# Row 1's front issued beside row 0's products, two rows' gating on GpSimd, and row steps placed at other times, in a kernel of time mixing and routed experts on one core

## The chip, the cores and the metric

The kernel runs on one core of one Trainium2 chip. The metric is the time of one execution on the device in microseconds; the median of three runs stands for a kernel. The engines are TensorE (PE; its weight loads are PEld), VectorE (DVE), ScalarE (ACT), GpSimd (POOL) and SyncE (SP, which issues most of the transfers).

## What is computed

The input x is 16 rows of 512 tokens with 256 channels, in float32. Two layers follow each other, both of the form x + layernorm(layer(layernorm(x))):

```python
x = x + layernorm(attn(layernorm(x)))
x = x + layernorm(ffn(layernorm(x)))
```

The first layer (attn) shifts a quarter of the channels by one token forward and a quarter backward, mixes this with the unshifted tokens in three ways, projects to k, v and r, and runs a recurrence over the tokens:

```python
eku = exp(u + kt); out = (a + eku * vt) / (b + eku)
ek = exp(kt);      a, b = a * ew + ek * vt, b * ew + ek
...
return (sigmoid(r) * out) @ Wo.T
```

The second layer (ffn) routes each token to the best two of eight experts (gate by softmax, 256 channels to 256 hidden, silu(x w1 + b1) * (x w3 + b3), then w2), and adds a shared expert with 512 hidden channels that every token goes through.

## The kernel before, in words

A row (b = 0 to 15, 512 tokens, 256 channels) is the unit of the first layer. The tokens lie in four tiles of 128, the channels in two halves of 128. The work of a row has a front and a back, each a list of named steps; a third kind of work fills in between.

**The front** (`front`, L289): `sum` and `sq` (L293 to L316) find mean and variance of the tokens: for row 0 on DVE, for the others on ACT with accumulated sums, with small operations on POOL (`scales`, L263). `xn` normalises on ACT (L278, called from L318). `pt` transposes on PE (L284) and ACT copies to `xx` (shifted) and `x1` (L329 to L332). `mix` makes `d`, `mk`, `mv`, `mr` on DVE (L334 to L341). `k0` and `k1` (`kv`, L356) each project k and v for one half of the channels (PE L346, two matmuls of 512 columns each), take exp of k on ACT (`ek`, L364), multiply by v on DVE (`ekv`, L366) and run two scans on DVE (`sb`, `sa`, L371), whose first columns POOL sets to zero. `r` projects r and takes exp on ACT (`er`, L352). `d0` and `d1` (`divide`, L374) are two DVE operations and a reciprocal (L379) for one half; `f0` and `f1` (`finish`, L381) are one DVE operation and the product `g` (L384).

**The back** (`back`, L395): `po0` and `po1` multiply g by Wo, 8 matmuls each (L406), with the statistics on DVE (`st_b`, L253). `x2` normalises on ACT and POOL adds x (L421). `stc` takes the statistics of the sum (`st_c`) and POOL makes the scales. `xr` normalises on ACT into a tile that also holds gate weight and destination of each token; `pu` transposes that tile (PE) and ACT copies it to `xT`; `pl` and `pg` (L461, L473) make the gate's logits and turn them; the top two and the counts follow on DVE (L479 to L494); `pc` (L499) ranks the tokens on PE, DVE makes their places in a buffer in HBM (L502 to L515), and POOL scatters the rows there with 8 indirect transfers (L520). `sel` chooses the blocks of 256 tokens of one expert that are full by then.

**What fills in between.** `shared` (L722) is the shared expert of one row in six steps: four of two times four matmuls of 512 columns (`hs_pa`, `hs_pb`, L734) and two of `pz` (L749). An expert block is pushed through a pipeline (`push`, L704): the block is loaded, turned (`px`, L648), multiplied by w1 and w3 (`pa`, `pb`, L662), gated on ACT (`sil`, L665) and DVE (`he`, L667), multiplied by w2 (`pq`, L678), biased on DVE (`ye`, L682), weighted on ACT and scattered by POOL (L691). A push of one block does px of that block, pq of another and pa, pb of the first. BESIDE says how many shared steps go beside each of the first rows.

**What sets the order.** PE, DVE, ACT and SP execute their instructions in the order in which the program writes them (`manual_schedule`, L106); POOL's are chained to the same order by `pool()` (L143). The program collects every step with a time and calls the steps sorted by that time (`at`, `in_order`, L889 to L895). Row b begins at START[b] or PERIOD behind the one before; `ROW` gives the offset of each step of any row, `ROWS` what is other for single rows (L32, L33). `CONST_AT` places a step that makes small constants (`the_constants`, L206: iota on POOL, casts and memsets on DVE), `WHOLE_AT` one that scales three weights (`whole_weights`, L237). The times are no microseconds: only the order that they give matters. Behind the last row's front comes the tail: remaining blocks, shared steps at the times in FILL, and the end of each half row (`fetch`, `gather`, `conclude`, `put`; K_FIRST and K_LAST place them), which reads the experts' results, adds, normalises and writes out.

**Tiles.** The pool `wk` has one buffer for each tag (`d`, `mk`, `mv`, `mr`, `xx`, `xn`, `g`, `ek0`, `sb0` and so on; `hs0` and `hs1` belong to the shared expert), so that a row's tile must be read to its end before the next row's is written. Three x tiles are in turn. PSUM is a pool of eight banks that all products share.

Of the kernel before, what the change touches and what calls it, by code (L numbers as in the profile page):

```python
# [8 lines left out]
F32 = mybir.dt.float32  # L9
# [19 lines left out]

PERIOD = 10.0  # L30
START = [0.0, 10.0, 20.0, 30.0, 40.0]
ROW = {'x': -7.6, 'sum': -5.31, 'sq': -4.3, 'xn': -1.7, 'pt': -0.59, 'mix': 0.8, 'r': 3.2, 'k0': 2.61, 'k1': 2.82, 'd0': 3.51, 'f0': 7.4, 'd1': 7.41, 'f1': 7.42, 'po0': 9.6, 'po1': 12.6, 'x2': 12.91, 'stc': 12.92, 'xr': 17.9, 'pu': 19.21, 'pg': 19.52, 'pc': 20.43, 'sel': 21.5, 'pl': 19.22}  # L32
ROWS = {1: {'x': -8.3, 'sum': -5.6, 'sq': -4.51, 'xn': -2.5, 'pt': -1.99, 'mix': 0.0, 'r': 6.0, 'd0': 6.01, 'f1': 9.8, 'po0': 11.4, 'po1': 12.4, 'x2': 14.11, 'stc': 14.21, 'xr': 18.1, 'pu': 19.91, 'pg': 20.33, 'pc': 20.84, 'sel': 20.85, 'pl': 20.22}, 3: {'xn': -0.1, 'pt': 0.01, 'mix': 1.3, 'f0': 7.0, 'd1': 7.01, 'f1': 8.3, 'po0': 11.39, 'po1': 11.4, 'x2': 11.41, 'stc': 11.42, 'xr': 16.0, 'pu': 17.61, 'sel': 21.2, 'pl': 17.92}, 0: {'x': -7.1, 'sum': -5.11, 'sq': -1.1, 'xn': -1.09, 'pt': -1.08, 'mix': -1.07, 'r': 6.6, 'k0': -0.29, 'k1': 0.12, 'd0': 6.61, 'f0': 6.62, 'd1': 6.63, 'f1': 7.6, 'po0': 12.59, 'x2': 12.71, 'stc': 12.72, 'xr': 17.6, 'pu': 19.31, 'pg': 20.32, 'pc': 21.83, 'sel': 21.84, 'pl': 19.32}, 2: {'sq': -3.51, 'xn': -3.5, 'd0': 3.71, 'f0': 5.9, 'd1': 5.91, 'f1': 7.2, 'po0': 10.6, 'po1': 11.6, 'x2': 11.91, 'stc': 12.52, 'xr': 16.6, 'pu': 16.91, 'pc': 20.23, 'sel': 21.2, 'pl': 16.92}}  # L33
CONST_AT = 8
WHOLE_AT = -3.8
X_PARTS = 2
VSTATS = 1
LEAD = 1
TURN_FIRST = True
PHASE = 0.2  # L40
BESIDE = [9, 6, 5, 2]
EARLY = 7
LAST_BESIDE = 6
XR_COPY = "pool"
HALVES_AT = 2.5
FILL = [-0.7, 0.7, 1.2, 13.5, 14.0, 15.5]
Z_AFTER = [2, 3]
K_FIRST = 1.0
K_LAST = 32.4
FINE = 2  # L50
FETCH = 4.8
# [13 lines left out]
def kernel(  # L65
# [30 lines left out]


    full = [max(0, -((E * (BS - 1) - 2 * T * (b + 1)) // BS)) for b in range(B)]
    LEFT = (2 * N - E) // P + E - 2 * full[B - 2]
    SINGLE = E - 1  # L100
    PAIRS = -((SINGLE - LEFT) // 2)
# [187 lines left out]
    def front(b):  # L289
# [32 lines left out]
        def turn():  # L322
            xn = it.pop("xn")
            p0 = it["p0"] = transposed(xn, 0, f"pt0_{b}")
            p1 = transposed(xn, 1, f"pt1_{b}")
            xx = it["xx"] = wk.tile([P, T], F32, tag="xx", name=f"xx{b}")
            pool(nc.gpsimd.memset(xx[:H, 0:1], 0.0))
            pool(nc.gpsimd.memset(xx[H:P, T - 1 : T], 0.0))
            nc.scalar.copy(xx[:H, 1:T], p0[:H, 0 : T - 1])  # L329
            nc.scalar.copy(xx[H:P, 0 : T - 1], p0[H:P, 1:T])  # L330
            x1 = it["x1"] = wk.tile([P, T], F32, tag="x1", name=f"x1_{b}")
            nc.scalar.copy(x1, p1)  # L332

        def mix():  # L334
            d = wk.tile([P, T], F32, tag="d", name=f"d{b}")
            nc.vector.tensor_tensor(d, it["p0"], it["xx"], ALU.subtract)
            it["m"] = {}
            for n, c in (("k", C_MK), ("v", C_MV), ("r", C_MR)):
                m = wk.tile([P, T], F32, tag=f"m{n}", name=f"m{n}{b}")
                nc.vector.scalar_tensor_tensor(m, d, colt[:, c : c + 1], it["xx"], ALU.mult, ALU.add)  # L340
                it["m"][n] = m  # L341

# [38 lines left out]
        def finish(o):  # L381
            ek, ekv, sa, sb = w[o]
            nc.vector.scalar_tensor_tensor(sa, ekv, eu[:, o : o + 1], sa, ALU.mult, ALU.add)
            nc.vector.tensor_mul(gs[b][:, o, :], sa, sb)  # L384

        return dict(
            sum=sums, sq=squares, xn=norm, pt=turn, mix=mix, r=receptance, k0=lambda: kv(0), k1=lambda: kv(1),
# [710 lines left out]
```

## Time and profile before

| what | value |
|---|---|
| median of 3 runs | 1077.15 us (1076.97 to 1079.2) |
| the profiled execution's own time | 1082.54 us |
| its span | 1080.8 us |
| PE busy | 1012.6 us (94%), 4202 matmuls |
| PEld busy | 701.4 us (65%) |
| DVE busy | 769.2 us (71%) |
| ACT busy | 541.5 us (50%) |
| POOL busy | 569.2 us (53%) |
| mean granted clock of PE | 0.979 |

A span is the time from the first to the last instruction; the execution's own time lies 1.7 us around it. Starts in the timeline are microseconds from the span's start. A row of the timeline is start, duration of the group, engine, line, operation, output and inputs, shape, the count of instructions in the group (xN), and in brackets the idle time before it with what released the engine. The granted clock is the share of the full TensorE clock, 1.00 or 0.50 at any moment, as a mean over the stretch asked for.

### The profile page before, as it was taken

The page shows a single profiled execution, that of the slowest core. Times are in us where ns is not written, and L with a number is a line of the kernel's source. Part 1 is how long each engine was busy: PE and PEld are TensorE (multiplying, and loading weights), DVE is VectorE, ACT ScalarE, POOL GpSimd, SP SyncE. Part 2 cuts the span into 40 slices and gives each one's busy share as a digit, 9 for nine tenths or more (in the row PEclk, how much of TensorE's full clock was granted, in tenths as well). Part 3 has the DMA queues.
Part 4 walks back from the last instruction along what each step waited for, and adds up shares of the span by engine and source line. Part 5 has one row for each costly group of instructions (what it writes and reads, how often), then busy time and mean ns, then how long its engine had stood idle before and what let it go on. Part 6 is the DMA issues. An engine that isn't in the chain of part 4 may idle for free.

```text
span 1080.8 us, 15095 instructions
## 1 busy us (share of the span) xinstructions
PE 1012.6 (94%) x4202; PEld 701.4 (65%) x4202; DVE 769.2 (71%) x1905; ACT 541.5 (50%) x1150; POOL 569.2 (53%) x858
## 2 busy tenths in 40 slices
PE   5769898999999999999999999989999999999996
PEld 2335454767777677866768676667667878556554
DVE  4897696887797888878888887866353222478864
ACT  3355463657557484755757566543423333333341
POOL 2336435174656547465654646554442222369885
PEclk9789999999999999999999999989999999999998
DMA  4011313436465554645556464543556766879943
GB/s 161 6 39 38 112 71 126 151 120 192 146 200 159 175 186 154 215 153 169 154 184 189 163 192 156 171 162 119 164 196 217 246 217 207 282 246 314 314 143 114
DMA packets 80900, 181.68 MB, mean 168 GB/s; under 512 B 9597, under 2 KB 45583, under 8 KB 80816
## 3 DMA queue, kind: packets, MB, share of 16 engines
q1 hardware_dynamic: 67360, 144.89, 42.0%
q0 software_dynamic: 12736, 34.77, 8.7%
q10 hardware_dynamic: 720, 1.06, 0.3%
q8 instruction: 33, 0.54, 0.2%
q14 instruction: 51, 0.42, 0.1%
HBM read 123.12 MB, written 58.47 MB: 168 GB/s over the span
## 4 chain that ended last, share of the span: by engine, by line
PE 67%; issue 5%; ACT 4%; DVE 3%; POOL 3%; DMA 2%; SPq 0%; DVEq 0%; POOLq 0%; ACTq 0%
PE pq L678 10%; PE pa L662 9%; PE pz L749 8%; PE hs_pa L734 8%; PE pb L662 8%; PE hs_pb L734 7%; PE po L406 4%; PE pv L346 3%; PE pk L346 3%; PE pr L346 3%; PE px L648 2%; POOL xbuf L520 1%; DVE he L667 1%; PE pt L284 1%; ACT xr L278 1%
## 5 line engine op out<-in xcount | busy, mean ns | idle before, releaser
L691 POOL DMA_INDIRECT ybuf<-ye,xg x135 | 137.5, 1019 | 235.2 <-ACT ye L689 176.1
L520 POOL DMA_INDIRECT xbuf<-xr,place x128 | 134.7, 1052 | 94.3 <-DVE rest L515 46.7
L678 PE MATMUL pq<-we,he 128*128 128x256 f32 x540 | 134.2, 391 | 12.6 <-DVE he L667 11.8
L662 PE MATMUL pa<-xgT,we 128*128 128x256 f32 (+1 forms) x568 | 130.0, 372 | 0.0
L667 DVE SCALAR_TENSOR_TENSOR he<-pb,we,sil 128x256 f32<-128x256 f32 (+1 forms) x142 | 60.0, 463 | 96.7 <-PE pb L662 59.6
L662 PE MATMUL pb<-xgT,we 128*128 128x256 f32 (+1 forms) x568 | 128.3, 369 | 0.0
L734 PE MATMUL hs_pa<-xT,ws1t 128*128 128x512 f32 x256 | 120.6, 593 | 0.0
L734 PE MATMUL hs_pb<-xT,ws3t 128*128 128x512 f32 x256 | 120.3, 592 | 0.0
L678 PEld LDWEIGHTS pq<-we,he 128*128 128x128 f32 x540 | 97.6, 193 | 31.2 <-DVE he L667 17.4
L665 ACT ACTIVATE sil<-pa,we 128x256 f32<-128x256 f32 (+1 forms) x142 | 58.0, 460 | 117.7 <-PE pa L662 77.9
L749 PE MATMUL pz<-ws2t,hs 128*128 128x256 f32 x512 | 115.8, 380 | 0.2 <-DVE hs L740 0.2
L662 PEld LDWEIGHTS pa<-xgT,we 128*128 128x128 f32 x568 | 106.1, 193 | 14.2
L662 PEld LDWEIGHTS pb<-xgT,we 128*128 128x128 f32 x568 | 104.1, 190 | 13.2
L749 PEld LDWEIGHTS pz<-ws2t,hs 128*128 128x128 f32 x512 | 96.7, 190 | 19.8 <-issue 5.7
L379 DVE RECIPROCAL sb<-sb 128x512 f32<-128x512 f32 x32 | 107.3, 3353 | 1.1
L734 PEld LDWEIGHTS hs_pb<-xT,ws3t 128*128 128x128 f32 x256 | 48.6, 190 | 61.2 <-issue 56.7
L740 DVE SCALAR_TENSOR_TENSOR hs<-hs_pb,colt,hs_s 128x512 f32<-128x512 f32 x64 | 46.5, 733 | 51.9 <-PE hs_pb L734 21.7
L734 PEld LDWEIGHTS hs_pa<-xT,ws1t 128*128 128x128 f32 x256 | 48.3, 190 | 43.7 <-issue 40.1
L278 ACT ACTIVATE acc<-acc,nb_d,rs_d 128x256 f32<-128x256 f32 x64 | 34.9, 593 | 81.1 <-POOL nb_d L273 80.9
L682 DVE TENSOR_TENSOR ye<-pq,we 128x512 f32<-128x512 f32 (+1 forms) x71 | 46.7, 658 | 36.1 <-PE pq L678 31.8
L364 ACT ACTIVATE ek<-pk 128x512 f32<-128x512 f32 x32 | 18.9, 597 | 102.3 <-PE pk L346 53.7
L406 PE MATMUL po<-wa,g 128*128 128x256 f32 x256 | 63.1, 391 | 5.0 <-DVE g L384 4.9
(187 smaller groups left out, 1868.7 us busy)
## 6 DMA issues: line engine op xcount, KB each, us to landing
we<-in_we SPq DMA_DIRECT2D x71, 898.0 KB
xg<-xbuf SPq DMA_DIRECT2D x64, 258.0 KB
in<-ybuf SPq DMA_DIRECT2D x32, 512.0 KB
x<-in_x SPq DMA_DIRECT2D x15, 512.0 KB
out<-acc SPq DMA_DIRECT2D x30, 256.0 KB
x2s<-x SPq DMA_DIRECT2D x14, 512.0 KB
inx<-x2s SPq DMA_DIRECT2D x19, 256.0 KB
zs<-z SPq DMA_DIRECT2D x9, 512.0 KB
```

The source lines that it names most:

```text
L346: nc.tensor.matmul(p, w[:, c, o * P : (o + 1) * P], r, start=(c == 0), stop=(c == NC - 1))
L379: nc.vector.reciprocal(sb, sb)
L406: nc.tensor.matmul(p[:, i, :], g[:, c, t * P : (t + 1) * P], woT[:, c, :], start=(c == 0), stop=(c == NC - 1))
L520: i = nc.gpsimd.indirect_dma_start(out=xbuf[:, :], out_offset=bass.IndirectOffsetOnAxis(ap=place[:, t, k : k + 1], axis=0), in_=xr[k][:, t ...
L662: nc.tensor.matmul(p[:, f, :], w[:, k : k + P], xgT[:, c, :], start=(c == 0), stop=(c == NC - 1))
L665: nc.scalar.activation(s[:, f, :], pp[0][:, f, :], AF.Silu, bias=w[:, O_B1 + f : O_B1 + f + 1])
L667: nc.vector.scalar_tensor_tensor(h[:, f, :], pp[1][:, f, :], w[:, O_B3 + f : O_B3 + f + 1], s[:, f, :], ALU.add, ALU.mult)
L678: nc.tensor.matmul(p[:, t, :], h[:, f, t * P : (t + 1) * P], w[:, k : k + C], start=(f == 0), stop=(f == NF - 1))
L682: nc.vector.tensor_tensor(y, p, w[:, None, O_B2 : O_B2 + C].to_broadcast([P, n, C]), ALU.add)
L691: j = nc.gpsimd.indirect_dma_start(out=ybuf[:, :], out_offset=bass.IndirectOffsetOnAxis(ap=xg[:, t, R_TO : R_TO + 1].bitcast(U32), axis=0) ...
L734: nc.tensor.matmul(p, w[:, c, f * P : (f + 1) * P], xT[:, c, :], start=(c == 0), stop=(c == NC - 1))
L749: nc.tensor.matmul(p[:, i, :], h[f][:, t * P : (t + 1) * P], ws2t[:, f, :], start=(f == 0), stop=(f == NS - 1))
```

## The change

Row 1's `sum`, `sq`, `xn`, `pt` and `mix` are issued before row 0's `r` and `d0`, where only its `sum` and `sq` were before; its `k0` and `k1` go ahead of row 0's `po0` and `po1`, behind which they were. Since row 0's `mk`, `mv`, `mr`, `xx` are still being read then, row 1 has tiles of its own for them, with the tags `hs0` and `hs1`, which the shared expert does not use yet. For rows 0 and 1 the product `g` (four instructions) is issued on POOL instead of DVE (`G_POOL`). The constants are made before the weights are scaled, at the start, not behind row 0's products.

The other numbers place steps anew. Each x is loaded one place earlier. In row 1's back, shared steps stand between `pg` and `pc`, and `pl`, `pg` follow `pu` without row 3's `pt` between; in row 2's, `pg` and `pc` stand directly behind each other and ahead of a shared step that was between them before. In rows 4 to 14 `x2` and `stc` of the row before go ahead of `k1`, and `f0` goes ahead of an expert block; the order on PE is the same there. Row 15's `r` and `d0` come two time units later, so that on DVE two blocks' `ye` and `he` stand ahead of its division, and on ACT two loads of a function table are added. In the tail one shared step comes one push earlier, `pc` of row 15 stands behind both `pz` of one row instead of between them, and a few of the first gathers are 0.2 earlier. `FIRST_CHOICE` is 0 and changes nothing.

```diff
@@ -29,23 +29,25 @@
 
 PERIOD = 10.0
 START = [0.0, 10.0, 20.0, 30.0, 40.0]
-ROW = {'x': -7.6, 'sum': -5.31, 'sq': -4.3, 'xn': -1.7, 'pt': -0.59, 'mix': 0.8, 'r': 3.2, 'k0': 2.61, 'k1': 2.82, 'd0': 3.51, 'f0': 7.4, 'd1': 7.41, 'f1': 7.42, 'po0': 9.6, 'po1': 12.6, 'x2': 12.91, 'stc': 12.92, 'xr': 17.9, 'pu': 19.21, 'pg': 19.52, 'pc': 20.43, 'sel': 21.5, 'pl': 19.22}
-ROWS = {1: {'x': -8.3, 'sum': -5.6, 'sq': -4.51, 'xn': -2.5, 'pt': -1.99, 'mix': 0.0, 'r': 6.0, 'd0': 6.01, 'f1': 9.8, 'po0': 11.4, 'po1': 12.4, 'x2': 14.11, 'stc': 14.21, 'xr': 18.1, 'pu': 19.91, 'pg': 20.33, 'pc': 20.84, 'sel': 20.85, 'pl': 20.22}, 3: {'xn': -0.1, 'pt': 0.01, 'mix': 1.3, 'f0': 7.0, 'd1': 7.01, 'f1': 8.3, 'po0': 11.39, 'po1': 11.4, 'x2': 11.41, 'stc': 11.42, 'xr': 16.0, 'pu': 17.61, 'sel': 21.2, 'pl': 17.92}, 0: {'x': -7.1, 'sum': -5.11, 'sq': -1.1, 'xn': -1.09, 'pt': -1.08, 'mix': -1.07, 'r': 6.6, 'k0': -0.29, 'k1': 0.12, 'd0': 6.61, 'f0': 6.62, 'd1': 6.63, 'f1': 7.6, 'po0': 12.59, 'x2': 12.71, 'stc': 12.72, 'xr': 17.6, 'pu': 19.31, 'pg': 20.32, 'pc': 21.83, 'sel': 21.84, 'pl': 19.32}, 2: {'sq': -3.51, 'xn': -3.5, 'd0': 3.71, 'f0': 5.9, 'd1': 5.91, 'f1': 7.2, 'po0': 10.6, 'po1': 11.6, 'x2': 11.91, 'stc': 12.52, 'xr': 16.6, 'pu': 16.91, 'pc': 20.23, 'sel': 21.2, 'pl': 16.92}}
-CONST_AT = 8
-WHOLE_AT = -3.8
+ROW = {'x': -9.6, 'sum': -5.31, 'sq': -4.3, 'xn': -2.2, 'pt': -0.59, 'mix': 0.9, 'r': 3.2, 'k0': 2.61, 'k1': 2.82, 'd0': 3.51, 'f0': 6.4, 'd1': 7.41, 'f1': 7.42, 'po0': 9.6, 'po1': 12.6, 'x2': 12.81, 'stc': 12.82, 'xr': 17.8, 'pu': 19.11, 'pg': 19.42, 'pc': 20.43, 'sel': 21.4, 'pl': 19.12}
+ROWS = {1: {'x': -11.09, 'sum': -11.08, 'sq': -11.07, 'xn': -10.56, 'pt': -9.61, 'mix': -9.6, 'r': 5.0, 'k0': 1.71, 'k1': 1.82, 'd0': 5.11, 'f0': 7.0, 'd1': 7.01, 'f1': 9.5, 'po0': 11.1, 'po1': 12.4, 'x2': 14.11, 'stc': 14.21, 'xr': 17.8, 'pu': 19.61, 'pg': 19.73, 'pc': 20.24, 'sel': 20.25, 'pl': 19.72}, 3: {'xn': -0.4, 'pt': 0.01, 'mix': 1.3, 'f0': 7.0, 'd1': 7.01, 'f1': 8.3, 'po0': 11.39, 'po1': 11.4, 'x2': 11.41, 'stc': 11.42, 'xr': 16.0, 'pu': 17.61, 'sel': 21.2, 'pl': 17.92}, 0: {'x': -7.1, 'sum': -5.61, 'sq': -1.6, 'xn': -1.59, 'pt': -1.58, 'mix': -1.07, 'r': 3.6, 'k0': -0.29, 'k1': 0.12, 'd0': 3.61, 'f0': 3.62, 'd1': 3.63, 'f1': 7.6, 'po0': 12.59, 'x2': 12.71, 'stc': 12.72, 'xr': 17.6, 'pu': 19.31, 'pg': 20.32, 'pc': 21.83, 'sel': 21.84, 'pl': 19.32}, 2: {'x': -7.3, 'sum': -5.01, 'sq': -3.21, 'xn': -3.2, 'd0': 3.41, 'f0': 5.6, 'd1': 5.61, 'f1': 6.9, 'po0': 10.8, 'po1': 11.7, 'x2': 12.01, 'stc': 12.42, 'xr': 16.5, 'pu': 17.31, 'pg': 19.92, 'pc': 20.03, 'sel': 21.0, 'pl': 17.32}, 15: {'r': 5.2, 'd0': 5.51}}
+CONST_AT = -4
+WHOLE_AT = -1.8
 X_PARTS = 2
 VSTATS = 1
 LEAD = 1
 TURN_FIRST = True
 PHASE = 0.2
 BESIDE = [9, 6, 5, 2]
+G_POOL = 2
+FIRST_CHOICE = 0
 EARLY = 7
 LAST_BESIDE = 6
-XR_COPY = "pool"
+XR_COPY = 'pool'
 HALVES_AT = 2.5
-FILL = [-0.7, 0.7, 1.2, 13.5, 14.0, 15.5]
+FILL = [-0.7, 0.7, 1.2, 12.5, 14.0, 15.5]
 Z_AFTER = [2, 3]
-K_FIRST = 1.0
+K_FIRST = 0.8
 K_LAST = 32.4
 FINE = 2
 FETCH = 4.8
@@ -96,6 +98,9 @@
 
 
     full = [max(0, -((E * (BS - 1) - 2 * T * (b + 1)) // BS)) for b in range(B)]
+    for b in range(B - 1):
+        if b < FIRST_CHOICE:
+            full[b] = 0
     LEFT = (2 * N - E) // P + E - 2 * full[B - 2]
     SINGLE = E - 1
     PAIRS = -((SINGLE - LEFT) // 2)
@@ -323,7 +328,11 @@
             xn = it.pop("xn")
             p0 = it["p0"] = transposed(xn, 0, f"pt0_{b}")
             p1 = transposed(xn, 1, f"pt1_{b}")
-            xx = it["xx"] = wk.tile([P, T], F32, tag="xx", name=f"xx{b}")
+            if b == 1:
+
+                two = [wk.tile([P, 2, T], F32, tag=f"hs{i}", name=f"row1_{i}") for i in range(2)]
+                it["own"] = [two[i // 2][:, i % 2, :] for i in range(4)]
+            xx = it["xx"] = it["own"][3] if b == 1 else wk.tile([P, T], F32, tag="xx", name=f"xx{b}")
             pool(nc.gpsimd.memset(xx[:H, 0:1], 0.0))
             pool(nc.gpsimd.memset(xx[H:P, T - 1 : T], 0.0))
             nc.scalar.copy(xx[:H, 1:T], p0[:H, 0 : T - 1])
@@ -335,8 +344,8 @@
             d = wk.tile([P, T], F32, tag="d", name=f"d{b}")
             nc.vector.tensor_tensor(d, it["p0"], it["xx"], ALU.subtract)
             it["m"] = {}
-            for n, c in (("k", C_MK), ("v", C_MV), ("r", C_MR)):
-                m = wk.tile([P, T], F32, tag=f"m{n}", name=f"m{n}{b}")
+            for i, (n, c) in enumerate((("k", C_MK), ("v", C_MV), ("r", C_MR))):
+                m = it["own"][i] if b == 1 else wk.tile([P, T], F32, tag=f"m{n}", name=f"m{n}{b}")
                 nc.vector.scalar_tensor_tensor(m, d, colt[:, c : c + 1], it["xx"], ALU.mult, ALU.add)
                 it["m"][n] = m
 
@@ -381,7 +390,10 @@
         def finish(o):
             ek, ekv, sa, sb = w[o]
             nc.vector.scalar_tensor_tensor(sa, ekv, eu[:, o : o + 1], sa, ALU.mult, ALU.add)
-            nc.vector.tensor_mul(gs[b][:, o, :], sa, sb)
+            if b < G_POOL:
+                pool(nc.gpsimd.tensor_tensor(gs[b][:, o, :], sa, sb, ALU.mult))
+            else:
+                nc.vector.tensor_mul(gs[b][:, o, :], sa, sb)
 
         return dict(
             sum=sums, sq=squares, xn=norm, pt=turn, mix=mix, r=receptance, k0=lambda: kv(0), k1=lambda: kv(1),
```

## The prediction

> **What bounds the kernel now.** I read the page's slices first, then the table by stretches, the waits of PE, and the timeline where a wait is long.
>
> ```profile
> PE   5769898999999999999999999989999999999996
> PEclk9789999999999999999999999989999999999998
> ```
>
> A digit is a fortieth of the span, 27 us. PE is full in nearly every slice; the thin ones are the first three or four, one after 700 us, and the last. Stretches (start:end, length, PE, PEld, DVE, ACT, POOL busy, then the granted clock):
>
> ```profile
> 0.00:27.00 27.00, 15.42 (x32) 6.88 (x32) 12.96 (x31) 10.54 (x29) 6.01 (x25) 1.00 0.49 161
> 27.00:54.00 27.00, 19.04 (x48) 10.45 (x48) 23.55 (x42) 9.92 (x24) 8.66 (x15) 0.75 0.01 5
> 54.00:81.00 27.00, 16.37 (x69) 9.89 (x68) 24.41 (x58) 13.68 (x28) 8.49 (x19) 0.81 0.12 38
> ...
> 300.00:400.00 100.00, 98.70 (x465) 71.85 (x464) 83.36 (x206) 62.53 (x138) 58.76 (x87) 1.00 0.57 177
> ...
> 712.00:716.00 4.00, 0.00 (x0) 0.00 (x0) 4.00 (x3) 0.15 (x1) 2.99 (x5) 0.92 0.09 33
> 716.00:720.00 4.00, 3.74 (x9) 3.02 (x10) 0.60 (x2) 1.23 (x3) 2.21 (x3) 0.50 0.41 120
> ```
>
> In 27 to 81 DVE is busy (24 of 27 us), not PE: row 0's chain runs alone. From the first shared product (73.53) PE is the bound (98.7 of 100), and whatever DVE, ACT or POOL save there buys nothing unless PE waits for it. PE executes the same matmuls after the change, and the same set stands ahead of the first shared product. So the time moves by three things only: when the first shared product starts, how long PE waits after it, and how long its clock is halved (0.50 above, behind a wait). PE's waits after 80 us (total, times, longest):
>
> ```profile
> PE pq L678 <- DVE he L667: 11.8, 24, 4.3
> PE pr L346 <- ACT x L278: 4.4, 1, 4.4
> PE pl L461 <- ACT xT L446: 3.9, 14, 0.8
> PE pg L473 <- ACT lg L469: 2.2, 3, 1.4
> PE pc L499 <- DVE sc L494: 1.1, 1, 1.1
> ```
>
> The two waits of 4.3 and 4.4 us, and the row-1 waits of pg and pc, are all that steps of named rows can win.
>
> **1. The front, up to 73.53.** The path, start and duration:
>
> ```profile
> 26.75 0.72 DVE L377 SCALAR_TENSOR_TENSOR sb<-ek,eu,sb 128x512 f32<-128x512 f32 x1
> 28.31 3.35 DVE L379 RECIPROCAL sb<-sb 128x512 f32<-128x512 f32 x1
> ...
> 38.41 0.69 DVE L384 TENSOR_TENSOR g<-sa,sb 128x512 f32<-128x512 f32 x1
> ...
> 39.16 5.14 PE L406 MATMUL po<-wa,g 128*128 128x256 f32 x14 [4.92 <-DVE g L384]
> ...
> 48.51 4.35 POOL L421 TENSOR_TENSOR x<-x,x 128x512 f32<-128x512 f32 x2 [1.06 <-ACT x L278]
> ```
>
> - *ACT.* Row 1's sums (1.7 from 22.60), squares (2.1), normalising (2.1) and POOL's scales between them now precede row 0's exp ek: 20.8 instead of 18.14. Its product ekv waited for pv until 20.35 anyway, so DVE's scans of row 0 end 27.25 instead of 26.83: +0.4.
> - *Row 1's mix* (0.69+0.75+0.75+0.74, 2.8 with overlap) now precedes row 0's division: its first stt starts at about 30.05, +3.3. The constants' casts and memsets (39.02 to 40.17, 1.1) go to the start, beside DVE's wait for weights; without that cover they cost 1.1.
> - *g on POOL.* Division and finishing took 26.75 to 39.10. Without two multiplies of 0.65 they take 11.05, to 41.1. A POOL multiply of this size is not in the trace; nearest is POOL's add (L421, same shape): median 1.27, 2.17 each in the row above, where DVE's scan of two SBUF inputs runs beside (2.22 against 1.20 alone). DVE runs row 1's scans here now. Bounds 1.27 to 2.2: g at 42.5 to 43.3.
> - The Trainium skill, "SBUF — State Buffer", section "Who interferes with whom", speaks against this edit: a DVE instruction with two SBUF inputs and a GpSimd instruction reading SBUF exclude each other. By it part 1 ends at its upper end, which is rival A below; the slowed pair agrees.
> - *po, statistics.* Row 1's ekv and scans (2×2.87) go ahead of the statistics, to 46.9, beside POOL's g and po (5.8 us at half clock). po ends at 48.3, the statistics at 49.3 to 50 (45.5 before).
> - *Given back.* Those scans no longer run beside the two adds of x2: 1.27 each instead of 2.17. Row 0's second statistics end at 56.0 to 56.7, not 54.06.
> - From there the chain (scales, row 2's squares and normalising, xr, pu, pl, pg, top-2, pc) took 19.47; 18.4 to 19.5 now, row 1's g being out of it. First shared product 74.4 to 76.2. **Taken: +1.8**; bounds −2 (DVE's 2.8 us of multiplies all come back) to +4.5 (upper POOL price, po wholly at half clock).
>
> **2. Row 1's pl, pg, pc (108 to 123).** The waits for pg (1.42) and pc (1.07) get shared products or transposes in front of them. pl now waits for xT behind row 3's normalising on ACT (1.7), pg 0.5. Counting from pu to the third shared step: 122.79 becomes 121.45. **−1.3** (0 to −2.5). The windows there show clock 1.00, so no clock comes back.
>
> **3. Row 3's r (182 to 187).** pr waits 4.42 for ACT's normalising of x2, which frees PSUM banks, which waits for POOL's nb_b, behind eight scatters (168.63 to 178.96). What counts is when row 2's places are ready. Row 2's pg and pc move ahead of a shared step, so DVE makes the places earlier; a new wait of some 2.7 us appears between pg and pc, the top-2 (112.64 to 115.40 for row 1) being uncovered, but POOL's chain ends 1.8 to 2 us sooner against PE's work. The 4.42 shrinks accordingly, and the half-clock stretch behind it (0.66 in 182:187, worth 1.7) goes or moves. px, 187.20 before, comes 3.55 sooner, of which part 2 is 1.3. **−2.25** (−4 to +0.8, where both waits stay).
>
> **4. Rows 4 to 14.** PE's order is the same. On DVE and ACT x2's statistics go ahead of the second scan pair, f0 goes ahead of an expert block's he, and each x load (512 KB) goes ahead of the block loads' SP instructions of a place or two; PE waits for a load once only in the whole run (px for xg, 1.0 us), so this costs nothing, or up to 1 us where it pushes such a load. f0 (0.65+0.69) goes into time in which DVE waited for pb (59.6 us, 26 times). PE's bank releases move: pk's and pv's banks 4 to 6 us later. **0**; bounds −2 to +7.
>
> **5. Row 15's division (711 to 730).**
>
> ```profile
> 711.92 3.35 DVE L379 RECIPROCAL sb<-sb 128x512 f32<-128x512 f32 x1
> ...
> 715.74 0.86 DVE L667 SCALAR_TENSOR_TENSOR he<-pb,we,sil 128x256 f32<-128x256 f32 x2
> 716.26 3.78 PE L678 MATMUL pq<-we,he 128*128 128x256 f32 x8 [4.34 <-DVE he L667]
> 719.83 3.06 PE L662 MATMUL pa<-xgT,we 128*128 128x256 f32 x8
> ```
>
> The division (0.72+0.69+3.35) stands ahead of he. Afterwards he is ahead of it, but behind row 14's statistics (2.75) and the scans moved behind them; he at about 714.3, pq at 714.85, gap 2.6. Before, the clock was halved 715.6 to 722.5, which costs 3.4 of PE work; behind the shorter gap 0 to 1.7. The next pq waits 0.65 more. pu comes at 726.35, not 730.54. ACT reloads a table twice more (1.28), off the path. **−4.2** (−1 to −6).
>
> The Trainium skill, "TensorE: Matmul & The Clock Gate", section "What's actually happening", lets the clock fall after an idle window of about 3.4 us: by it 2.6 us would leave the clock whole, which is rival E below. The trace does not bear it out: a wait of 2.19 us ending at 806.88 was followed by a clock of 0.63 (808:812), so I go by that row.
>
> **6. Tail.** One shared step moves by a push, pc.15 behind a pz, some gathers by 0.2: **0** (±1). The 10 us behind the last matmul stay.
>
> **Sum:** 1.8−1.3−2.25+0−4.2+0 = −5.95. The profiled execution took 1082.54 (span 1080.8), so 1076.6. The unprofiled median, 1077.15, is 5.4 lower; PE's order is the same in both, so I take the difference over: **1071.2**.
>
> **Rivals.**
> - *A: the front costs more* (POOL's g at 2.2, po at half clock): +4.5 instead of +1.8: 1073.9. For: scans run beside g. Against: adds are shortened by the same edit. 0.12.
> - *B: row 15's wait is only shortened* and the clock stays halved as long: −1.4 instead of −4.2: 1074.0. For: the row at 806.88. 0.14. A and B together 1076.7: 0.08.
> - *C: the front gains* (DVE, busy 24 of 27 us, loses 2.8 us of multiplies): −2: 1067.4. Against: row 0's division waits for row 1's mix. 0.10.
> - *D, slower:* in rows 4 to 14 f0's 1.34 us on DVE delays he, and PE's pq waits, eleven times. For: pq already waits for he 24 times. Against: DVE's 59.6 us of waiting for pb. At 1 us a row it is +11: 1082.2; it turns the sum slower from 0.74 us a row ((5.95+2.15)/11). 0.16.
> - *E: the clock stays whole* behind row 15's wait of 2.6 us: all 3.4 come back, part 5 is −5 and the time 1070.4. For: waits of 1.42 and 1.07 cost no clock. Against: the one of 2.19 did. 0.07.
> - *The change doesn't do what it says* for row 1: its early products do not start shared work earlier, since row 0's path sets it. That is my own case; it needs no price.
>
> **How the numbers follow.** My forecast has 0.33, E 0.07, A 0.12, B 0.14, both 0.08, C 0.10, D 0.16. About 0.2% (2.15 us) is what a measurement can tell from no change: faster means under 1075.0, slower over 1079.3. Faster: 0.33, E 0.07, C 0.10, 0.08 of A, 0.10 of B: 0.68. Same: the rest of A and B (0.08), both together 0.08, 0.02 of D: 0.18. Slower: 0.14 of D. The range 1066 to 1078 holds all but D and an end of C.
>
> **What would show it.** First shared product at 75.3; POOL's g at 1.3 to 2.2 each; row 1's third shared step 1.3 sooner relative to the first; row 3's pr wait under 3 us and no clock below 0.9 behind it; row 15's pq wait 2.6 and its clock half for less than 3.5 us. I am wrong if the rows 4 to 14 change their length, if the first product comes before 72 or after 78, or if the pr wait stays at 4.4.

## The result

The changed kernel takes **1072.49 us** (median of 6 runs, 1071.29 to 1073.87), the kernel before in runs beside it 1078.75 (6 runs, 1076.97 to 1079.8): a ratio of 0.9945, 95% interval 0.9934 to 0.9955, or 5.9 us less. Forecast were 1071.2 and 5.95 less. A second set of runs of the same two kernels (below) gave 0.996 (0.9945 to 0.9974).

The profiled execution took 1072.72 us with a span of 1071.0. The two page rows that the prediction began with now read:

```profile
PE   5649998999999999999999999999999999999996
PEclk9869999999999999999999999999999999999998
```

The dip after 700 us is gone; in the second to fourth slices PE is no busier than before. The table by stretches of the changed kernel (columns as in the prediction):

```profile
27.00:54.00 27.00, 18.34 (x44) 9.24 (x42) 22.81 (x27) 4.58 (x10) 5.42 (x11) 0.87 0.00 1
54.00:81.00 27.00, 13.98 (x59) 9.07 (x60) 19.97 (x51) 15.45 (x37) 10.63 (x19) 0.62 0.12 40
...
300.00:400.00 100.00, 98.70 (x464) 71.92 (x463) 85.35 (x217) 62.54 (x136) 59.29 (x86) 1.00 0.59 185
```

PE is busy for 32.3 us in 27 to 81, where it was for 35.4 before, at a clock that is halved for less of the first stretch (0.87, before 0.75) and more of the second (0.62, before 0.81); the steady stretch is the same to 0.01 us. What PE waited for after 80 us in the changed kernel (total, times, longest):

```profile
PE pq L690 <- DVE he L679: 6.5, 26, 0.6
PE pl L473 <- ACT xT L458: 4.8, 14, 1.7
PE pc L511 <- DVE mine L505: 2.7, 1, 2.7
PE px L660 <- ACT ye L701: 1.2, 1, 1.2
...
PE px L660 <- DMA xg<-xbuf: 1.1, 1, 1.1
```

The 4.4 of row 3's r is gone from this list, a pc with 2.7 stands in it, and no pq waits longer than 0.6.

Since PE is full, the time can be followed by marks on it. The profiled execution of before, from which the prediction was made, turned out to have 4 us more between 785 and 898 us than another one of the same kernel (before_third, told below). Both are in this table of starts on PE in us (the last row is the end of the last matmul, then the execution's own time), with the difference of the changed kernel to each:

| mark | before | before_third | changed | difference |
|---|---|---|---|---|
| first shared product | 73.53 | 73.91 | 76.28 | +2.75, +2.37 |
| first px, behind row 3's r | 187.20 | 188.08 | 186.04 | −1.16, −2.04 |
| row 13's pg | 682.38 | 683.22 | 680.69 | −1.69, −2.53 |
| row 15's pg | 784.09 | 784.53 | 778.25 | −5.84, −6.28 |
| last matmul's end | 1070.19 | 1066.47 | 1060.35 | −9.84, −6.12 |
| the execution | 1082.54 | 1078.81 | 1072.72 | −9.82, −6.09 |

So the front costs, rows 1 to 3 give back more than that, and row 15 gives the largest piece, as forecast. The last step of the first difference, −4, is no gain of the change. The other traces of before differ by 2 us too: in before_again row 15's pg comes at 781.72, as its wait there is 3.63 us and one stretch of half clock follows it, not two.

The front of the changed kernel, in a timeline (start, duration, engine, line, operation):

```profile
29.98 0.75 DVE L386 SCALAR_TENSOR_TENSOR sb<-ek,eu,sb 128x512 f32<-128x512 f32 x1
...
35.64 1.64 POOL L394 TENSOR_TENSOR g<-sa,sb 128x512 f32<-128x512 f32 x1 [16.69 <-DVE sa L392]
...
36.27 1.56 DVE L387 SCALAR_TENSOR_TENSOR sb<-er,sb 128x512 f32<-128x512 f32 x1
...
43.18 5.46 PE L418 MATMUL po<-wa,g 128*128 128x256 f32 x14 [5.15 <-POOL g L394]
...
53.28 2.49 POOL L433 TENSOR_TENSOR x<-x,x 128x512 f32<-128x512 f32 x2 [1.13 <-ACT x L283]
...
66.86 2.81 PE L289 MATMUL pu<-ident,xr 128*128 128x128 f32 x8 [14.78 <-ACT xr L283]
...
76.28 1.96 PE L746 MATMUL hs_pa<-xT,ws1t 128*128 128x512 f32 x4
```

Row 0's division starts at 29.98, behind row 1's mix; the two adds take 2.49 together, not 4.35; PE then stands still for 14.78 us.

### The profile page after: what moved, and what is told of

Its sections match the earlier page's. It is cut to its first block, busy times and chain, and to the rows that moved or that the text cites. A ratio compares the mean times of both kernels' runs of the same rounds, so it can differ in the third digit from the quotient of the medians.

```text
span 1071.0 us, 15081 instructions
## 1 busy us (share of the span) xinstructions
PE 1007.9 (94%) x4202; PEld 701.0 (65%) x4202; DVE 772.3 (72%) x1901; ACT 543.5 (51%) x1152; POOL 577.1 (54%) x862
## 4 chain that ended last, share of the span: by engine, by line
PE 79%; DVE 6%; issue 4%; POOL 4%; ACT 3%; DMA 2%; ACTq 0%; POOLq 0%; DVEq 0%; SPq 0%
PE pq L690 10%; PE pa L674 10%; PE hs_pa L746 10%; PE hs_pb L746 9%; PE pb L674 9%; PE pz L761 9%; PE pk L355 4%; PE po L418 4%; PE pv L355 4%; PE pr L355 4%; PE px L660 2%; PE pt L289 1%; POOL xbuf L532 1%; DVE he L679 1%; DMA wa<-in_wa 1%
## 5 line engine op out<-in xcount | busy, mean ns | idle before, releaser
L703 POOL DMA_INDIRECT ybuf<-ye,xg x135 | 142.4, 1055 | 214.7 <-ACT ye L701 170.0
L690 PE MATMUL pq<-we,he 128*128 128x256 f32 x540 | 131.0, 385 | 6.5 <-DVE he L679 6.5
L283 ACT ACTIVATE x<-po,nb_b,rs_b 128x256 f32<-128x256 f32 x64 | 30.9, 564 | 105.8 <-POOL nb_b L278 105.8
L258 DVE BATCH_NORM_STATS2 st_c<-x 128x6 f32<-128x256 f32 x64 | 26.2, 409 | 66.2 <-POOL x L433 65.3
L418 PE MATMUL po<-wa,g 128*128 128x256 f32 x256 | 67.2, 411 | 6.5 <-POOL g L394 6.5
```

The costliest lines, as they stand in the source:

```text
L283: nc.scalar.activation(dst, src, AF.Identity, bias=nb[:, t : t + 1], scale=rs[:, t : t + 1])
L418: nc.tensor.matmul(p[:, i, :], g[:, c, t * P : (t + 1) * P], woT[:, c, :], start=(c == 0), stop=(c == NC - 1))
L690: nc.tensor.matmul(p[:, t, :], h[:, f, t * P : (t + 1) * P], w[:, k : k + C], start=(f == 0), stop=(f == NF - 1))
L703: j = nc.gpsimd.indirect_dma_start(out=ybuf[:, :], out_offset=bass.IndirectOffsetOnAxis(ap=xg[:, t, R_TO : R_TO + 1].bitcast(U32), axis=0) ...
```

## The experiments

The kernels ran in three groups, each with runs of the kernel before beside it: front_old, g_dve, row15_old and pg2_early in the first, before_again, rows_old, po3_first and xr0_first in the second, the rest in the third. Each group ran on a chip of its own. The kernel before took 1079.07, 1081.69 and 1077.77 us in them, so medians of two groups are not compared without that; a ratio is to the kernel before in the same group. Each edit is to the changed kernel unless said.

### The front as before

```diff
 ROWS[0]
-'sum': -5.61, 'sq': -1.6, 'xn': -1.59, 'pt': -1.58, 'r': 3.6, 'd0': 3.61, 'f0': 3.62, 'd1': 3.63
+'sum': -5.11, 'sq': -1.1, 'xn': -1.09, 'pt': -1.08, 'r': 6.6, 'd0': 6.61, 'f0': 6.62, 'd1': 6.63
 ROWS[1]
-'sum': -11.08, 'sq': -11.07, 'xn': -10.56, 'pt': -9.61, 'mix': -9.6, 'k0': 1.71, 'k1': 1.82
+'sum': -5.6, 'sq': -4.51, 'xn': -2.5, 'pt': -1.99, 'mix': 0.0, 'k0': 2.61, 'k1': 2.82
...
-G_POOL = 2
+G_POOL = 0
...
-it["own"][i] if b == 1 else
+it["own"][i] if b == OWN else
```

(OWN is −1; row 1's r, d0 to f1 and po0 and the two placements of the constants and whole weights go back with them.)

> The changed kernel with the front of rows 0 and 1 in the order of before (row 1's normalising, turning and mixing behind row 0's division, row 1's k behind row 0's po, the constants behind row 0's products, g on DVE, no tiles of its own); all else as changed. Theory 1, from the two traces: the front part of the change costs 2.75 us (the first shared product came at 76.28 instead of 73.53) and gives nothing back later, since rows 1 to 3 are gained by the order of their backs. Then the first shared product is at 73.5 and the time is 2.75 us under the changed kernel's, about 1069.7, a ratio of 0.992 to before. Rival: row 1's early work is what lets rows 1 and 2 run without their old waits; then the first shared product is at 73.5, but a wait of 1 to 4 us comes back between it and row 4, and the time is within 1 us of the changed kernel's, 1072.5, or above.

Measured: 1069.55 us (4 runs, 1068.93 to 1071.43), ratio 0.991 (0.9893 to 0.9926), 2.9 us under the changed kernel's median, 3.8 us by the two ratios. On PE in its trace:

```profile
63.05 2.80 PE L290 MATMUL pu<-ident,xr 128*128 128x128 f32 x8 [9.46 <-ACT xr L284]
...
72.40 1.96 PE L747 MATMUL hs_pa<-xT,ws1t 128*128 128x512 f32 x4
```

The first shared product is 3.9 us earlier than in the first trace of the changed kernel; 2.1 of it are left at the first px and at row 13's pg, and 4.0 against the second trace, which like this one has half clock behind row 1's pl. Theory 1 holds: the part that names the change is a loss, and all of the gain is in the rest. Row 1's early front, the tiles and the constants went back together; only g was also tried alone. The first product also comes 1.1 earlier than in the kernel before, though row 0's order is the same there but for small moves (x loads, row 2's sums). At least half of this goes with the clock and not with the order: it is granted in full from 17.68 us on in this trace, and from 18.75, 19.04 and 19.55 in the three of before; row 0's first reciprocal then starts at 27.64, 28.18, 28.31 and 28.56, so half of each delay is handed on, and the first shared product at 72.40, 73.34, 73.53 and 73.91. So 0.5 to 0.9 us of the 3.9 is luck of this trace; whether the small moves bring the rest was not tried.

### g on DVE

```diff
-G_POOL = 2
+G_POOL = 0
```

> The changed kernel with all g multiplies on DVE; all else as changed. Theory 1: g on POOL takes 1.26 us against 0.69 and a hand-over, but frees DVE of two times 0.65 us ahead of row 0's statistics; put back, the first g comes in DVE's way, row 0's statistics end 1.3 us later and the first shared product is at 77.5 instead of 76.3: time 1073.8. Rival (the exclusion of POOL by DVE's operations with two SBUF inputs makes g on POOL a loss): the first shared product comes earlier than 76.0 and the time falls below 1072.

Measured: 1072.87 us (4 runs), ratio 0.9945 (0.9928 to 0.9962): no difference. In the trace po starts earlier, and the first shared product 0.4 later (76.69), not 1.2 later:

```profile
41.70 0.69 DVE L396 TENSOR_TENSOR g<-sa,sb 128x512 f32<-128x512 f32 x1
...
42.45 3.78 PE L418 MATMUL po<-wa,g 128*128 128x256 f32 x8 [5.43 <-DVE g L396]
```

Both theories missed. Row 0's second statistics end at 56.90 here and at 56.97 with g on POOL, so nothing came free for them. What POOL takes off DVE it gives back twice: its multiply takes 1.26 us against 0.69, and where it runs beside a DVE operation with two SBUF inputs both get longer, 1.64 on POOL and 1.56 instead of 0.69 on DVE (35.64 and 36.27 above). That DVE row is row 0's second division, on the path. The Trainium skill, "SBUF — State Buffer", section "Who interferes with whom", states that such a pair excludes each other; this row bears it out: POOL's multiply starts beside a DVE operation that ends at 36.15 and itself ends at 37.28, and the division, started at 36.27, ends 0.55 us behind that.

### Row 15's division at the old place

```diff
-15: {'r': 5.2, 'd0': 5.51}
```

> The changed kernel with row 15's r and division at the place of all rows again (ahead of two blocks' he). Theory 1: the wait of pq for he, 4.3 us, comes back, and the half-clock stretch behind it; the time rises by 3.75 us (what the two traces show between row 14 and the pz behind row 15) to 1076.2. Rival: the wait goes because row 14's statistics stand ahead of the scans, not because of row 15's step; then the wait stays under 2 us and the time rises by less than 1.5 us.

Measured: 1078.68 us (10 runs, 1076.74 to 1079.42), ratio 0.9991 (0.9982 to 1.0001): nearly all of the change's gain is lost with these two numbers. In its trace:

```profile
713.08 3.35 DVE L388 RECIPROCAL sb<-sb 128x512 f32<-128x512 f32 x1
...
716.35 0.63 DVE L694 TENSOR_TENSOR ye<-pq,we 128x512 f32<-128x512 f32 x1
716.89 0.86 DVE L679 SCALAR_TENSOR_TENSOR he<-pb,we,sil 128x256 f32<-128x256 f32 x2
...
717.42 3.78 PE L690 MATMUL pq<-we,he 128*128 128x256 f32 x8 [5.48 <-DVE he L679]
```

The wait is 5.48, longer than the 4.34 of before, as row 14's statistics and row 15's scans now stand ahead of the division too (711.51 is its first operation), and the clock is halved behind it as before. Theory 1 holds in kind, but the size is more than its 3.75. By the ratios it is 5.0 us against the first runs of the changed kernel and 3.3 against the second. In the traces, row 13's pg to row 15's pg takes 101.99 us here and 97.56 and 97.41 in the changed kernel.

### Row 2's pg ahead of a shared step

```diff
 ROWS[2]
-'pg': 19.92
+'pg': 19.0
```

> The changed kernel with row 2's pg ahead of a shared step instead of directly ahead of pc. Theory 1: the changed kernel's gain at row 3's r is not one of a wait less, but of a shorter wait: 2.71 us of pc for the top-2, which nothing covers, with a half-clock stretch (166.9 to 170.3, worth 1.7) behind it. With a shared step between pg and pc both go: 4.4 us less, 1068.1, no wait above 0.7 us between 120 and 250 us and no clock below 1.00 there. Rival: the wait only returns at row 3's r (it stood at 4.42 us before), as POOL's chain is what is late; then the time is within 1 us of 1072.5 and pr waits for ACT's x again.

Measured: 1073.48 us (10 runs), ratio 0.9959 (0.9946 to 0.9973): nothing gained, and nothing lost that the time would show. PE's waits between 120 and 250 us:

```profile
PE pr L355 <- ACT x L283: 4.3, 1, 4.3
PE pc L511 <- DVE mine L505: 0.7, 1, 0.7
```

The wait is back at row 3's r, with the size that it had before: the rival was right. Why shows in the rows of DVE and POOL of this run:

```profile
167.47 0.75 DVE L752 SCALAR_TENSOR_TENSOR hs<-hs_pb,colt,hs_s 128x512 f32<-128x512 f32 x1 [2.30 <-ACT hs_s L751]
...
170.14 0.17 DVE L525 CAST place<-pos 128x8 uint32<-128x8 f32 x1
...
170.60 1.10 POOL L532 DMA_INDIRECT xbuf<-xr,place  x1 [17.48 <-DVE rest L527]
```

The top-2 is done sooner here, but the shared step's operation hs stands between it and the places on DVE, and waits 2.30 us for ACT, which loads its table first. The places come 5.3 us behind the top-2 (`mine` at 164.86), in the changed kernel 2.6 (166.07, 168.68). From the places to pr everything is fixed, eight scatters, the scales and ACT's x: 13.8 us here, in the changed kernel and in the one before. A shared step between pg and pc covers PE and delays the chain on which PE waits next. The marks show a loss that the time does not: from the first shared product to the first px it is 113.50 us here and 111.31 in the second trace of the changed kernel, both with half clock behind row 1's pl. So the changed place of this step is worth some 2.2 us there.

### Row 3's po ahead of row 2's pc

```diff
 ROWS[3]
-'po0': 11.39, 'po1': 11.4
+'po0': 9.925, 'po1': 9.926
```

> The changed kernel with row 3's po0 and po1 ahead of row 2's pc. With a shared step between pg and pc the wait of 2.71 us only went to row 3's r (4.34 us, and no gain): POOL's chain (places, eight scatters of 1.27 us, the scales of row 3's x2) sets it. Theory 2: what binds is that the scales stand behind the scatters on POOL. With po ahead, its 3.7 us cover the top-2, the scales come ahead of the scatters, the banks come free 10 us earlier, and both waits go: 2.7 us and 1.7 of half clock, together 4.4: 1068.1, with no wait above 0.8 us between 150 and 200 us. Rival: another engine is as late as POOL there (DVE's places, or row 2's x2), and a wait of 2 us or more comes back within 30 us; then the gain is under 1.5 us.

Measured: 1077.43 us (10 runs, 1074.06 to 1080.5) where the kernel before took 1081.69, ratio 0.9954 (0.9936 to 0.9972). Both long waits are gone between 120 and 250 us, and two others are there:

```profile
PE pk L355 <- DVE mk L349: 1.7, 1, 1.7
PE pz L761 <- DVE hs L752: 1.1, 1, 1.1
```

The first px comes 3.1 us earlier than in the second trace of the changed kernel (184.81 against 187.89); 1.6 of it are left at row 13's pg (680.92 against 682.55). So POOL's scatters were what bound row 3's r, and DVE is little less late than POOL. By its time alone the run is not to be told from the changed kernel.

### The common steps of rows 4 to 15 as before

```diff
 ROWS[4] to ROWS[15]
+'x': -7.6, 'xn': -1.7, 'mix': 0.8, 'f0': 7.4, 'x2': 12.91, 'stc': 12.92, 'xr': 17.9, 'pu': 19.21, 'pl': 19.22, 'pg': 19.52, 'sel': 21.5
```

> The changed kernel with the steps of rows 4 to 15 that all rows share at the places of before (x2's statistics behind the second scan pair, f0 behind the expert block, x loads a place later); front, rows 1 to 3, row 15's division and the tail as changed. Theory 1: PE hides these moves; the time stays within 1 us of the changed kernel's 1072.5 and the length from row 6 to row 14 does not change by more than 0.5 us. Rival: they take part in closing row 15's gap (row 14's statistics ahead of row 15's scans); then the wait of pq in row 15 is over 2 us again, though the division stays late, and the time rises by 2 to 5 us.

Measured: 1082.61 us (10 runs, 1078.34 to 1086.81), ratio 1.0011 (0.9992 to 1.0029): the whole gain is lost. Neither theory said so. Against the second trace of the changed kernel the first px is 3.15 us later (191.04), row 13's pg 4.2. The rows, ACT at row 4's sums, PE at row 2's pu, and PE in row 15:

```profile
147.69 0.42 ACT L307 ACTIVATE xn<-x 128x256 f32<-128x256 f32 x1 [2.32 <-DMA x<-in_x]
...
152.49 0.33 PE L289 MATMUL pu<-ident,xr 128*128 128x128 f32 x1 [0.84 <-ACT xr L283]
...
724.30 0.69 PE L660 MATMUL px<-ident,xg 128*128 128x128 f32 x4 [2.86 <-DMA xg<-xbuf]
```

Row 4's x is issued on SP at 139.37 there, behind a block's load, and at 114.38 in the first trace of the changed kernel; ACT waits 2.32 us for it, row 2's xr stands behind that on ACT, pu starts late (0.84) and the clock falls behind it (0.50 in 156 to 158). In row 15 pq has no wait above 0.6 us, so the late division suffices for that; but a block's tokens arrive 2.86 us late, and the clock is halved behind that wait too. Which of the eleven numbers bring this second wait was not tried. The first belongs to the x load. In the kernel before the load has the same place behind a block's load, and is issued at 132.04 without such a wait; so it is beside the changed order of rows 0 to 3 that it comes too late.

### Row 0's xr ahead of row 2's normalising

```diff
 ROWS[0]
-'xr': 17.6
+'xr': 16.795
 ROWS[1]
-'po0': 11.1
+'po0': 12.1
```

> The changed kernel with row 0's xr on ACT between row 2's squares and row 2's normalising instead of behind both, and row 1's po0 behind the first shared step. In the changed kernel's trace PE is idle from 52.07 to 66.86, waiting for xr, whose scales are there at 59.8; ACT waits 2.15 us for POOL in between. Theory 1: pu starts at 62.7 instead of 66.9, the first shared product at 72 instead of 76.3, and all of it stays: 1068.3. Rival: row 1's po0 and row 2's k, which need DVE, are as late; the first shared product comes 4 us sooner, but a wait of 2 to 4 us appears before 110 us, and the time stays above 1071.

Measured: 1073.36 us (5 runs) where the kernel before took 1081.69, ratio 0.9934 (0.9909 to 0.9959). On PE:

```profile
62.70 2.81 PE L289 MATMUL pu<-ident,xr 128*128 128x128 f32 x8 [10.97 <-ACT xr L283]
...
72.86 0.60 PE L511 MATMUL pc<-mine,before 128*128 128x8 f32 x2 [2.71 <-DVE mine L505]
...
73.74 3.76 PE L746 MATMUL hs_pa<-xT,ws1t 128*128 128x512 f32 x4
```

pu starts at 62.70, as forecast to the digit; the first shared product gains 2.5 us, not 4.3, since pc now waits 2.71 for the top-2 with nothing beside it. Row 13's pg is 1.4 earlier than in the first trace of the changed kernel. Each theory has half.

### The two kernels again

> The kernel before, unchanged, for a second trace. The profiled execution of before took 1082.54, 3.5 us over the median of its runs, and has a wait of 2.19 us at 806.88 behind an ACT that stood idle for 9 us, with a half-clock stretch behind it, which no trace since shows. Theory 1: this is an event of that one execution; then no wait of PE above 1 us lies between 740 and 900 us, the time is near 1079, and the waits at row 3's r (4.4) and row 15's pq (4.3 to 5.5) are there again. Rival: it belongs to the order of before; then it recurs at about the same place, and the change takes 4 us there.

> The changed kernel, unchanged, beside the next two on one chip, and for a second trace. Where the traces differ in the tail, SP's eight issues of the blank rows took 9.3 us in some and 14.4 to 15.6 us in others, whatever the kernel, and with the long ones PE waited 2.1 to 2.9 us near 800 us. Theory 1: that goes with the execution or the chip, not with the order; then this run has it whenever the kernel before has it beside it, the two traces differ by 3 to 6 us up to 790 us, and the ratio is 0.9945 again (0.993 to 0.996). Rival: the changed order keeps the tail free of it; then the issues take 9.3 us here and 15 us in the kernel before.

> The kernel before, unchanged, for a third trace, on the chip of the run before this one. Theory 1: the issues of the blank rows take as long as in the changed kernel on this chip (within 2 us); first shared product at 73.3, wait at row 3's r 4.4, at row 15's pq 3.6 to 4.3. Rival: 15 us here, 9.3 there.

The changed kernel took 1074.1 us (5 runs, 1072.28 to 1075.71), the kernel before 1077.77 (10 runs), ratio 0.996 (0.9945 to 0.9974). The two traces of before took 1078.49 and 1078.81 us; all three have row 3's wait (4.42 to 4.44), and row 15's is 4.34, 3.63 and 4.20. For the second trace of before both theories missed: the wait near 800 us came again (2.09 at 804.41), this time without half clock behind it, and in the third trace it is gone. For the other two runs theory 1 was right, with the ratio at the end of its range and the third trace's first product at 73.91, not 73.3.

The long wait near 800 us does not go with the order. SP issues eight transfers of blank rows there; from the first start to the last end this took 15.6 us in the profile of before, 15.2 in before_again, and 14.4 to 14.5 in the three changed orders of the same group, and every one of these five traces has a wait of pq of 2.1 to 2.9 us near 800. In the nine other traces it took 9.3 to 9.6 us, and no pq waits over 0.6 us there. SP's row in the changed kernel:

```profile
789.27 9.34 SPq L639 DMA_DIRECT2D xbuf<-blank  x8
```

before_third has 9.59, beside 9.32 in after_again. All traces of a group agree, so it goes with where or when a group runs. What makes the issues slow stays open.

### The best of both

```diff
 the front as before, and
-G_POOL = 0
+G_POOL = [1]
 ROWS[0]
-'xr': 17.6
+'xr': 16.795
 ROWS[1]
-'po0': 11.4
+'po0': 12.1
```

> The changed kernel with the front of rows 0 and 1 as before, but row 1's g on POOL, row 0's xr between row 2's squares and row 2's normalising, row 1's po0 behind the first shared step. Front as before was worth 3.0 us alone; xr earlier was worth 1.4 us at row 4 and 2.8 at row 15 in the changed kernel. Theory 1: both add where DVE lets them: row 1's second finish on DVE ends at about 67 and the top-2 follows it, so the first shared product is at 70 to 71; ratio 0.989 (1067 where the kernel before takes 1079). Rival: DVE is the limit of both, and the two are the same gain seen twice: ratio 0.991 as with the old front alone.

> The same with row 3's po0 and po1 ahead of row 2's pc too, which gave 1 to 2 us by row 14 alone. Theory 1: ratio 0.988, 1 us under the kernel without it. Rival: a wait for row 4's mix (1.67 us in the trace of that edit alone) and for hs takes all of it; no difference beyond 0.5 us.

Measured: 1069.63 us (5 runs, 1067.91 to 1073.06), ratio 0.9917 (0.9903 to 0.9932), for the first; 1068.23 (5 runs, 1065.67 to 1068.62), ratio 0.9902 (0.9886 to 0.9917), with row 3's po ahead too. The first is no better than the old front alone (0.991), as the rival had it. On PE in the second:

```profile
60.77 2.80 PE L290 MATMUL pu<-ident,xr 128*128 128x128 f32 x8 [5.68 <-ACT xr L284]
...
71.77 0.57 PE L512 MATMUL pc<-mine,before 128*128 128x8 f32 x2 [3.84 <-DVE sc L507]
...
72.61 3.76 PE L747 MATMUL hs_pa<-xT,ws1t 128*128 128x512 f32 x4
```

xr and pu come 2.3 us sooner than with the old front alone, and the first shared product not at all (72.61 against 72.40): the top-2 on DVE waits for row 1's finish, which ends at 69.1 in the first of the two, and pc stands 3.84. That the first product gains nothing is in part the clock at the start again: it is full from 19.83 and 19.70 us on in these two traces and from 17.68 in that of the old front alone, and in the same order row 0's second reciprocal starts at 34.86 and 34.79 instead of 33.79. By the ratios, each beats the kernel before and the changed kernel beside it (0.996). Their intervals overlap with each other's and with that of the old front alone, so what is shown is that the kernels with this front are better, not the order among the three.

## Why the prediction was right, point by point

The time and the sum came out (−5.95 forecast, −5.9 to −6.3 measured, −4.3 in the second set), the terms less exactly. The front cost 0.6 to 0.95 us more than forecast, row 3's r and rows 4 to 14 gave 0.75 more, and row 15 came out at or just under its term. That the sum fitted to 0.4 us is in part luck: single stretches of half clock, worth 1.7 us each, come or stay away from one trace to the next.

1. *Front: +1.8 forecast, +2.37 to +2.75 measured.* Nearly every start of the chain came within 0.3 us: ek 20.67 (20.8 forecast), the division 29.98 (30.05), po 43.18 (42.5 to 43.3), row 0's second statistics' end 56.97 (56.0 to 56.7), the adds 2.49 together. The rest was a part of the chain that I gave 18.4 to 19.5 us and that took 19.3. One row was missing: the mutual delay of POOL's first g and DVE's second division (1.56 instead of 0.69). I had looked for it only beside the scans. Undoing the front gave 2.9 us back by the medians.
2. *Row 1's back: −1.3 forecast, −1.38 between the first and the third row's work in the first trace* (the k product of row 3, 131.4 before and 132.8 after, with the front's 2.75 taken off). What I left out is the clock. The wait of pl, 1.67 us, halves it behind it in six of eight traces, which costs 1.7 and more than eats the gain; in the first trace of the changed kernel it did not, in the second it did (the third number from the end is the clock: 1.00 and 0.76):

```profile
112.00:116.00 4.00, 2.78 (x22) 1.29 (x23) 2.89 (x15) 2.76 (x5) 0.49 (x3) 1.00 0.42 170
```

```profile
112.00:116.00 4.00, 2.47 (x19) 1.26 (x20) 2.77 (x11) 3.06 (x6) 0.78 (x3) 0.76 0.34 138
```

   The second trace is 1.8 us behind the first at row 3's k product and still at row 13's pg, 0.3 of it from the front, and the second ratio is higher than the first by 0.0015, or 1.6 us.
3. *Row 3's r: −2.25 forecast, −2.5 measured (from −1.38 to −3.91 of the front's mark, at the first px).* The step was right in its end and half wrong in its way. The new wait of 2.71 at pc is there as forecast, but I counted it as off the path and POOL's chain as 1.8 to 2 us earlier. The places came 0.7 us earlier against PE's work (168.17 and 168.68, where pl stands at 150.04 and 151.23). The other 1.7 are the clock: the half-clock stretch lies behind pc now, in time in which PE would otherwise wait for POOL at r, and no longer behind r. In best1's trace that stretch is missing, and there pr waits 1.71 for ACT's x. Undone alone, the step cost 2.2 us by the marks.
4. *Rows 4 to 14: 0 forecast, −0.5 measured* (a wait of 0.75 of row 5's pl, at 256.45 before, is gone). Rival D did not come: pq waits 26 times, 0.6 at most. But "this costs nothing" of the x loads was wrong the other way round: with the changed rows 0 to 3 they are needed, and without these steps' new places the change is worth nothing (1.0011).
5. *Row 15: −4.2 forecast, −3.75 to −4.15 at row 15's pg, and 3.3 to 5.0 us by the ratios when it is taken away alone.* pq's wait is 0.64, not 2.6: row 14's statistics start at 704.60 and not at 708.04, twice as much earlier as row 13's pg (1.69). So rivals B and E were never put to the test there:

```profile
710.33 0.87 DVE L679 SCALAR_TENSOR_TENSOR he<-pb,we,sil 128x256 f32<-128x256 f32 x2
...
710.86 2.00 PE L690 MATMUL pq<-we,he 128*128 128x256 f32 x8 [0.64 <-DVE he L679]
...
712.70 3.35 DVE L388 RECIPROCAL sb<-sb 128x512 f32<-128x512 f32 x1
...
717.55 0.63 PE L660 MATMUL px<-ident,xg 128*128 128x128 f32 x4 [1.24 <-ACT ye L701]
```

   The division lies beside pa and pb here, and 1.24 us of wait are left behind it. Both traces of the changed kernel also have a half-clock stretch of some 3.4 us behind row 14's pu and pl (726.5 to 730 in the first), which seven of the eight other traces with this step do not have; it hides 1.7 us of the gain. From row 13's pg to row 15's pg it is 95.7 to 96.3 us in those seven, 97.56 and 97.41 in the two of the changed kernel, and 99.53 to 101.71 in the three of before; without the stretch the piece would have been larger than its term.
6. *Tail: 0 forecast, 0 measured* (−6.28 at row 15's pg and −6.12 at the end, against before_third). The profile from which I worked had 4 us of its own there. I took its distance to the median, 5.4 us, over unchanged, and this was right only because I took no gain out of that stretch.

Rival C failed in sign: the front did not gain. Rival A had the right sign, and the cost in a different row than the one that it named. "The change doesn't do what it says" came nearest to the truth: what names the change, row 1's front and g on POOL, is a loss of some 3 us and nothing else.

## What to carry to other kernels

When one engine is full from some point on, a step's gain is read as marks on that engine: measure each stretch from mark to mark, and undo single steps, since a change of many steps can hold a loss that its sum does not show. Where an engine waits at the end of a chain on other engines, covering the wait with other work gains nothing if that work's own operations stand in the chain (here a shared step's hs ahead of the places). And take more than one trace of each kernel: 4 us near 800 us in that of before were not the order's, and a stretch of half clock can be in one trace of a kernel and not in the next.

## What the runs showed of the hardware

- **The clock changes on a grid of 3.41 us, and a short wait costs half clock or nothing by how the grid cuts it.** In each of the fourteen traces all changes of the clock lie a whole multiple of 3.41 us apart (74.92, 167.08, 170.49, 726.86 and 730.27 in the first of the changed kernel), and the grid lies otherwise against the span's start from one trace to the next. A halved stretch is one step of it or several, and one costs 1.7 us. Cut along its own grid, each trace gives windows for which PE's idle time can be summed (by the ends that the profile models for its matmuls). Between 80 and 1040 us, all 24 windows at full clock in which PE was idle for 1.93 us or more were followed by half clock; of those with 1.72 to 1.92 us, 4 of 8; of all with less, three (1.33, 1.07 and 0.97), each with a row's transposes `pu` in it, and these stay unexplained. The same wait of 2.71 us at row 2's pc lies in one window in the changed kernel and is cut in two in best1 (start:end, length, PE, PEld, DVE, ACT, POOL busy, then the clock):

```profile
163.66:167.08 3.42, 0.75 (x5) 0.75 (x6) 2.76 (x20) 2.71 (x5) 0.00 (x0) 1.00 0.00 0
167.08:170.49 3.41, 3.41 (x9) 2.70 (x8) 3.12 (x14) 0.00 (x0) 1.10 (x1) 0.50 0.01 2
```

```profile
159.78:163.19 3.41, 2.08 (x12) 1.23 (x10) 2.12 (x13) 1.89 (x5) 0.00 (x0) 1.00 0.00 0
163.19:166.61 3.42, 2.04 (x11) 1.89 (x12) 2.72 (x18) 1.47 (x2) 0.00 (x0) 1.00 0.00 0
166.61:170.02 3.41, 3.41 (x14) 2.44 (x13) 3.31 (x10) 0.00 (x0) 2.33 (x2) 1.00 0.12 43
```

   So the clock was halved behind this wait in 7 of 8 traces, behind row 1's pl (1.67) in 6 of 8, behind pq near 800 us (2.1 to 2.9) in 2 of 5, behind a block's load near 910 us (1.7 to 2.7) in 4 of 7, behind the waits of 1.42 and 1.07 in row 1 of before in none of three, and behind waits of 3.6 us and more, after 80 us, always. The Trainium skill, "TensorE: Matmul & The Clock Gate", section "What's actually happening", names an idle window of about 3.4 us and says that the window runs free of the kernel; the grid agrees with both, but the window need not be idle throughout: 1.93 us of it were enough here.
- **A POOL operation that reads SBUF and a DVE operation with two inputs in SBUF lengthen each other**: 1.64 and 1.56 us instead of 1.26 and 0.69, in both traces of the changed kernel and in the last two kernels.
- **Eight transfers issued on SP took 9.3 us in some groups of runs and 14.4 to 15.6 in others**, and the slower ones cost PE a wait of 2 us or more, whatever the order.
